# A selective-scan layer: new load order, diagonals from ScalarE's queue, gate behind the scan, 416 columns on VectorE

## The chip, the cores and the metric

The kernel runs on one core of one Trainium2 chip. The core has five engines: TensorE (PE; its weight loads are shown as PEld), VectorE (DVE), ScalarE (ACT), GpSimd (POOL) and SyncE (SP), which only issues transfers here. Each engine works through its own list of instructions in order and waits on semaphores for the others. Transfers between the chip's DRAM and the on-chip memory are issued from SP's or ScalarE's list and carried out by 16 DMA engines. The metric is the time of one execution on the device in microseconds; the number to be predicted is the median of the runs.

## What is computed

Two layers in a row on x of shape 32 x 96 x 56 x 56. Layer 0 is a convolution block (expand, depthwise, squeeze-and-excite, project). Layer 1, to which the change belongs, is a two-block selective scan over the 3136 tokens of each image. Cut to what matters:

```python
xs, z = jnp.split(h @ in_w, 2, axis=-1)            # h: normalised tokens, 192 channels each
xc = silu(causal 4-tap convolution of xs)
dbl = xc @ xproj_w                                  # 6 + 16 + 16 columns: dt, B, C
delta = softplus(dt @ dt_w + dt_b)
dA  = exp(delta[..., None] * A)                     # 192 channels x 16 states
dBx = delta[..., None] * Bm[:, :, None, :] * xc[..., None]
hstates[l] = dA[l] * hstates[l-1] + dBx[l]          # a scan along the tokens
y = einsum('blds,bls->bld', hstates, Cm) + Dp * xc
y = y * silu(z)
seq = seq + y @ out_w                               # two such blocks, then a batch norm
```

## The kernel before

**Units and tiles.** Each image's 3136 tokens are cut into four chunks of 784 (`LC`). One chunk in one of the two blocks is a unit; there are 256 units, in which the blocks alternate (the second runs three chunks behind the first). A unit has 192 channels x 16 states = 3072 rows, that is 24 tiles of 128 rows (`NT`). Tile t is (k, j, p): k, one of three groups of 64 channels (t // 8); j, one of four groups of four states; p, one of two halves of the channels. A tile's 128 rows are four states (`sg`) by 32 channels.

**Work on a tile.** `decay` (L921, ScalarE) makes dA = exp(delta x A) from the tile `deltab`, which holds delta of the channels copied to all four states. dBx comes in two ways. For three of four j GpSimd multiplies `ub` (delta x xc, likewise copied) with `B` (`inject`, L958, one instruction for both p). For j = 0 (`by_pe`: tiles 0, 1, 8, 9, 16, 17) TensorE computes it in 32 small matmuls (64 records in the trace) from `ut` and `diag`, a matrix with B on its diagonals (`fill`, L935). `scan` (L969, VectorE) runs the recurrence. The product with C is split by columns: the first `LP` = 400 tokens go to VectorE (`product`, L977, which reads a copy of C in PSUM made by ScalarE in `bring`, L946), the other 384 to GpSimd (`rest`, L985); one instruction covers both p. `reduce` (L1016, TensorE) sums over the states into `yps`, a single PSUM bank that `seed` (L1003, ScalarE) first fills with Dp x xc. After a group's eight tiles `gated` (L1027, VectorE) multiplies the sum with z.

**The order.** Everything is in one loop over steps `at`, one tile a step; `tc.manual_schedule()` keeps that order on every engine. At step `at` the loop issues the decay of the next tile (for j = 0 two to four steps ahead, in a borrowed `bx` buffer, L921 `bx<-deltab`), the GpSimd product of dBx of tile at + 4, the seed and reduction of tile at - 4, the gate of tile at - 5, the scan of tile `at`, the product of tile at - 1, TensorE's fill of tile at + 1, and then pieces of work for other units (`todo`: projections, normalisation and so on of the unit two ahead, the output of the unit before). The gate stands ahead of the scan: gate (at - 5), scan (at), product (at - 1).

**The loads.** `fetch`, at the end of each step, issues a tile's loads at fixed leads, all from SP's list: delta 9 steps ahead of its tile (L890, four pieces of 196 KB, tiles 0, 8 and 16), u 8 steps ahead (L890, four pieces of 196 KB, the same tiles), the diagonals 8 steps ahead of tile 0 (L894, one transfer of 120 rows x 12576 bytes), B 9 steps ahead (L899, four pieces of 98 KB, tiles 2, 4 and 6), C 5 steps ahead (L899, four pieces of 98 KB, tiles 0, 2, 4 and 6). I call them delta0, delta8, B2, C4 and so on by their tile. They read small DRAM buffers which the preparation of the unit has written: `bcd` (B and C), `deltad`, `ud`, and `bdiag`, into which six small transfers scatter B's values between zeros. There is one `diag` buffer, so its load waits until TensorE has filled tile 17 of the unit before; `deltab` and `ub` have two buffers, `B` three, `C` four.

**Semaphores of the loads.** The transfers issued by SP and ScalarE take eight semaphores in turn. Before a transfer is issued, its engine waits until the earlier transfer on the same semaphore has landed. The turns are dealt when the program is built. An engine that waits there issues nothing else of its list.

Of the kernel before, what the change touches and what calls it, by code (L numbers as in the profile page):

```python
# [19 lines left out]
B, C, H, W = 32, 96, 56, 56  # L20
# [4 lines left out]
NL, NS, DIN, RANK, KC = 2, 16, 192, 6, 4  # L25
LC = 784
HB = LC // 2
LP = 400
NQ = L // LC
RB = HB // W  # L30
DG = 8
# [3 lines left out]
NT = 2 * NB * SG  # L35
# [5 lines left out]
TB = 120  # L41
TOFF, TCOL, TSZ = (0, 120, 211, 301), (0, 120, 211, 302), (120, 91, 91, 91)
TW = TCOL[-1] + TSZ[-1]
TR = 8 * TW

PE_TILES = (0, 1)
FOLD = NCT - 1
# [12 lines left out]
def conv_mamba_kernel(ctx, tc, a, out):  # L60
    nc = tc.nc
    v, s, g, pe, sp = nc.vector, nc.scalar, nc.gpsimd, nc.tensor, nc.sync
# [41 lines left out]
    with ExitStack() as ph:  # L104
# [17 lines left out]
        def wtile(name, shape):  # L122
            return wts.tile(list(shape), F32, name=name, tag=name)
# [85 lines left out]
        diag = wtile("diag", [128, len(PE_TILES), 9, 32])  # L209
# [7 lines left out]
        for i in range(NHB):  # L217
            t = hp3.tile([128, H + 2, W + 2], F32, name=f"hpad{i}", tag=f"hpad{i}")
# [239 lines left out]
    with ExitStack() as ph:  # L458
# [17 lines left out]
        def wt(shape, tag, bufs, n):  # L476
            return work.tile(shape, F32, name=f"{tag}_{n}", tag=tag, bufs=bufs)
# [52 lines left out]
        for i in range(NL):  # L530
# [8 lines left out]
            for h in range(2):  # L539
                cols = slice(h * C, h * C + C)  # L540
                ps = bank(f"cw_{i}_{h}")
                for o in range(KC + 1):
                    to = ps[: C + 1, o * C : o * C + C]
# [16 lines left out]
        for h in range(2):  # L560
            for i in range(NL):
                to = wd[h * 64 + 2 * NS : h * 64 + 2 * NS + RANK, i, :, :]
# [6 lines left out]
        for k in range(NB):  # L569
            ps = bank(f"wf_{k}")  # L570
            for h in range(2):
                r = slice(h * 64, h * 64 + 64)
# [6 lines left out]
        g.memset(xn[C : C + 1, :], 1.0)  # L579
        none = once.tile([TB, TR + 2], F32, name="none", tag="none")  # L580
        v.memset(none, 0.0)
        zdram = ph.enter_context(tc.tile_pool(name="l1z", bufs=1, space=DRAM))
        bdiag = [zdram.tile([TB * (TR + 2)], F32, name=f"bdiag{i}", tag=f"bdiag{i}") for i in range(2)]
        for t in bdiag:
# [28 lines left out]
        def prepare(n):  # L613
# [148 lines left out]
            def scatter(h, e):  # L762
                bt, z = d["btt"], TSZ[-1]
                to = bdiag[n % 2].rearrange("(p r) -> p r", p=TB)[:, :TR].rearrange("p (e h x) -> p e h x", e=2, h=2)
                if e == 2:
# [107 lines left out]
        def place(t):  # L873
            k, r = divmod(t, 2 * SG)
            return k, r // 2, r % 2

        def fetch(at, tags):

            n, t = divmod(at, NT)
            if not 0 <= n < len(units):  # L880
                return
            k, j, p = place(t)
            d = data[n]
            for tag in tags:
                if tag in ("delta", "u"):
                    if j == 0 and p == 0:
                        to = d[tag, k] = wt([128, 2, LC], f"{tag}b", 2, f"{n}_{t}")
                        of = d[tag][2 * DB * k : 2 * DB * (k + 1), :].rearrange("(p m) l -> m p l", p=2)
                        for sg in (0, 2, 1, 3):
                            sp.dma_start(to[sg * DB : sg * DB + DB], of)  # L890
                elif tag == "diag":
                    if t == 0:
                        to = d["diag"] = wt([TB, TR], "diag", 1, n)
                        sp.dma_start(to, bdiag[n % 2][: TB * TR].rearrange("(p r) -> p r", p=TB))  # L894
                elif k == 0 and p == 0 and (tag, j) != ("B", PEJ):
                    to = d[tag, j] = wt([128, LC], tag, 3 if tag == "B" else 4, f"{n}_{t}")
                    c0 = "BC".index(tag) * NS + j * SN
                    for sg in (0, 2, 1, 3):
                        sp.dma_start(to[sg * DB : sg * DB + DB], d["bc"][c0 + sg : c0 + sg + 1, :].to_broadcast([DB, LC]))  # L899
# [3 lines left out]
        def by_pe(at):  # L903

            return place(at % NT)[1] == PEJ

        def lend(at):

            if by_pe(at) and at % 2 == 0:
                to = wt([128, 2, LC], "bx", 3, at)  # L910
                for p in range(2):
                    das[at + p] = to[:, p, :]

        def decay(at):

            n, t = divmod(at, NT)
            i, d = units[n][1], data[n]
            k, j, p = place(t)
            if not by_pe(at):
                das[at] = dpool.tile([128, 2 * 512], F32, name=f"da_{at}", tag="da")[:, :LC]  # L920
            s.activation(das[at], d["delta", k][:, p, :], AF.Exp, scale=acol[:, j, i, 2 * k + p : 2 * k + p + 1])  # L921
# [18 lines left out]
        def bring(at):  # L940
# [3 lines left out]
            if p == 1:  # L944
                cps[at] = cpool.tile([128, LP], F32, name=f"cp_{at}", tag="cp")
                s.copy(cps[at], data[n]["C", j][:, :LP])  # L946

        def beside(x):

            return x.unsqueeze(1).to_broadcast([128, 2, x.shape[-1]])  # L950

        def inject(at):

            n, t = divmod(at, NT)
            k, j, p = place(t)
            if p == 0 and j != PEJ:
                bx = wt([128, 2, LC], "bx", 3, at)
                g.tensor_mul(bx, data[n]["u", k], beside(data[n]["B", j]))  # L958
                for p in range(2):
                    bxs[at + p] = bx[:, p, :]  # L960

        def scan(at):

            n, t = divmod(at, NT)
            (c, i), d = units[n], data[n]
            k, j, p = place(t)
            if p == 0:
                hhs[at] = wt([128, 2, LC], "hh", 3, at)
            v.tensor_tensor_scan(  # L969
                hhs[at - p][:, p, :], das.pop(at), bxs.pop(at), state[i][:, t : t + 1] if c % NQ else 0.0,  # L970
                ALU.mult, ALU.add,
            )

        def product(at):

            if place(at % NT)[2] == 1:
                v.tensor_mul(hcs[at - 1][:, :, :LP], hhs[at - 1][:, :, :LP], beside(cps.pop(at)))  # L977

        def rest(at):
# [3 lines left out]
            if p == 1:  # L983
                hcs[at - 1] = wt([128, 2, LC], "hc", 3, at)
                g.tensor_mul(hcs[at - 1][:, :, LP:], hhs[at - 1][:, :, LP:], beside(data[n]["C", j][:, LP:]))  # L985

# [9 lines left out]
        def seed(at):  # L996

            n, t = divmod(at, NT)
            k, j, p = place(t)
            if j == 0 and p == 1:  # L1000
                i, d = units[n][1], data[n]
                yps[k] = ypool.tile([128, 512], F32, name=f"y_{n}_{k}", tag="y")
                s.activation(yps[k][:, :HB], d["xc"][:, k, :], AF.Copy, scale=dp[:, i, k, 1:2])  # L1003
# [25 lines left out]
        total = len(units) * NT  # L1029
# [12 lines left out]
        def ahead(at):  # L1042

            return (2, 1) if at % NT == 0 else (4, 3)
# [5 lines left out]
        with tc.manual_schedule():  # L1050
            for at in range(min(todo), max(todo) + 1):
                for m in (2, 4):
                    if 0 <= at + m < total and by_pe(at + m) and (at + m) % 2 == 0 and ahead(at + m)[0] == m:
                        lend(at + m)
                if 0 <= at + 4 < total:
                    inject(at + 4)
                for u, step in todo.get(at, ()):
                    if u < 0.05:
                        step()
                if 0 <= at - LAG < total:  # L1060
                    seed(at - LAG)
                if 0 <= at + 1 < total and not by_pe(at + 1):
                    decay(at + 1)
                for x in range(at, at + 5):
                    pair = x // 2 * 2
                    if 0 <= x < total and by_pe(x) and pair - ahead(pair)[x - pair] == at:
                        decay(x)
                if 0 <= at < total:
                    bring(at)
                for step in early.get(at, ()):  # L1070
                    step()
                if 0 <= at - LAG - 1 < total:
                    gated(at - LAG - 1)
                if 0 <= at < total:
                    scan(at)
                if 0 <= at - 1 < total:
                    product(at - 1)
                if 0 <= at - 2 < total:
                    save(at - 2)
                if 0 <= at < total:  # L1080
                    rest(at)
                if 0 <= at + 1 < total and by_pe(at + 1):
                    fill(at + 1)
                for u, step in todo.get(at, ()):
                    if 0.05 <= u < 0.08:
                        step()
                if 0 <= at - LAG < total:
                    reduce(at - LAG)
                for u, step in todo.get(at, ()):
                    if u >= 0.08:  # L1090
                        step()
                fetch(at + 9, ("delta",))
                fetch(at + 8, ("u", "diag"))
                fetch(at + 9, ("B",))
                fetch(at + 5, ("C",))


    with ExitStack() as ph:
# [76 lines left out]
```

## Time and profile before

| | |
|---|---|
| median of 3 runs | 18660.26 us (18648.78 to 18682.66) |
| the profiled execution | 18688.67 us, its span 18686.8 us |
| layer 0 | until about 3270 us |
| layer 1's units (first to last scan) | about 3476 to 18389 us |
| end (batch norm, output) | the last 290 us |
| DVE busy in the span | 16816.5 us (90%) |
| POOL busy in the span | 14627.0 us (78%) |
| ACT busy in the span | 14047.1 us (75%) |
| PE busy in the span | 15916.5 us (85%) |
| DMA in layer 1 | 0.76 of 16 engines, 186 GB/s |

The costliest groups of layer 1, from the page (line, engine, operation, out<-in, shapes, count | busy us, mean ns | idle time just before, and its releaser):

```profile
L958 POOL TENSOR_TENSOR bx<-ub,B 128x1568 f32<-128x1568 f32 x2304 | 8172.9, 3547 | 185.9 <-DMA B<-bcd 98.1
L969 DVE TENSOR_TENSOR_SCAN hh<-da,state,bx 128x784 f32<-128x784 f32 x3456 | 6312.4, 1839 | 54.4 <-ACT da L921 44.0
L985 POOL TENSOR_TENSOR hc<-hh,C 128x768 f32<-128x768 f32 x3072 | 5616.9, 1831 | 435.0 <-DVE hh L969 247.5
L921 ACT ACTIVATE da<-deltab,acol 128x784 f32<-128x784 f32 x4608 | 4243.3, 921 | 1046.4 <-DVE hh L969 1023.4
L977 DVE TENSOR_TENSOR hc<-hh,cp 128x800 f32<-128x800 f32 x3072 | 2952.1, 961 | 0.4 <-ACT cp L946 0.3
```

How to read it: the busy columns say how full an engine is over the whole span, so the first 3270 us, in which GpSimd does little, pull its 78% down. What a stall in layer 1 costs is read from a unit: which instruction waited, for whom, and what stood behind it on its engine. Transfers do not count as busy time; a wait of SP shows as a gap between its rows, or as a group of rows that takes longer than its pieces.

### The profile page before, as it was taken

The numbers are of one execution on the slowest core, as the hardware profiler recorded it, in microseconds if no ns is written. First come the engines' busy times: TensorE is split into PE (matmuls) and PEld (weight loads), VectorE is DVE, ScalarE is ACT, GpSimd is POOL, SyncE is SP. The second block draws the span as 40 slices with busy tenths as digits, with TensorE's granted clock in tenths as the row PEclk, the third lists the DMA queues.
The fourth block names the chain that finished last, engine by engine and source line by source line (L and its number), as shares of the span: only waits on it lengthen the run. The fifth ranks groups of instructions, "written<-read, shape, count | busy, mean of one in ns | idle before, by whom it ended". The sixth has DMA issues, their size and how long they took to land.

```text
span 18686.8 us, 503802 instructions
## 1 busy us (share of the span) xinstructions
PE 15916.5 (85%) x207422; PEld 8426.7 (45%) x207422; DVE 16816.7 (90%) x12627; ACT 14047.1 (75%) x26284; POOL 14627.0 (78%) x6382
## 2 busy tenths in 40 slices
PE   8999999888888888888888888888888888888882
PEld 4444444444444444444444444444444444444441
DVE  8888888699999999999999999999999999999993
ACT  4444444688888888888888888888888888888884
POOL 0000000599999999999999999999999999999994
PEclk9999999899999999999999999999999999999996
DMA  1000000577777777777777777777777777777778
GB/s 29 26 24 26 24 26 22 130 187 186 187 186 187 188 187 187 186 186 187 186 188 184 187 187 187 186 186 187 185 186 185 186 186 186 187 187 186 187 186 222
DMA packets 1615417, 2945.98 MB, mean 158 GB/s; under 512 B 696982, under 2 KB 910190, under 8 KB 1576006
## 3 DMA queue, kind: packets, MB, share of 16 engines
q1 hardware_dynamic: 1604470, 2875.15, 62.4%
q0 software_dynamic: 6656, 38.54, 1.0%
q8 instruction: 1627, 26.66, 0.6%
q14 instruction: 680, 5.57, 0.1%
q10 hardware_dynamic: 1984, 0.07, 0.0%
HBM read 2456.09 MB, written 455.82 MB: 156 GB/s over the span
## 4 chain that ended last, share of the span: by engine, by line
issue 25%; DMA 22%; PE 13%; DVE 12%; ACT 11%; SPq 10%; POOL 7%; POOLq 0%; ACTq 0%; DVEq 0%
DMA diag<-bdiag 8%; DVE hh L969 6%; PE bp L935 5%; SPq L899 4%; SPq L890 4%; DMA deltab<-deltad 4%; DMA ub<-ud 4%; DVE hc L977 3%; POOL bx L958 3%; DVE h L314 2%; DMA B<-bcd 2%; POOL hc L985 2%; ACT bx L921 2%; ACT da L921 2%; DMA C<-bcd 2%
## 5 line engine op out<-in xcount | busy, mean ns | idle before, releaser
L958 POOL TENSOR_TENSOR bx<-ub,B 128x1568 f32<-128x1568 f32 x2304 | 8172.9, 3547 | 185.9 <-DMA B<-bcd 98.1
L969 DVE TENSOR_TENSOR_SCAN hh<-da,state,bx 128x784 f32<-128x784 f32 x3456 | 6312.4, 1839 | 54.4 <-ACT da L921 44.0
L985 POOL TENSOR_TENSOR hc<-hh,C 128x768 f32<-128x768 f32 x3072 | 5616.9, 1831 | 435.0 <-DVE hh L969 247.5
L921 ACT ACTIVATE da<-deltab,acol 128x784 f32<-128x784 f32 x4608 | 4243.3, 921 | 1046.4 <-DVE hh L969 1023.4
L1016 PE MATMUL y<-hc,rel 128*32 128x392 f32 x24576 | 2866.3, 538 | 514.5 <-ACT y L1003 510.5
L935 PE MATMUL bp<-diag,ut 91*32 91x91 f32 (+1 forms) x98304 | 2980.0, 279 | 352.1 <-DVE hh L969 199.2
L935 PEld LDWEIGHTS bp<-diag,ut 91*32 91x32 f32 (+1 forms) x98304 | 2672.8, 123 | 1116.3 <-DVE hh L969 668.1
L977 DVE TENSOR_TENSOR hc<-hh,cp 128x800 f32<-128x800 f32 x3072 | 2952.1, 961 | 0.4 <-ACT cp L946 0.3
L389 POOL TENSOR_TENSOR x<-x,x 96x784 f32<-96x784 f32 x128 | 267.8, 2093 | 3079.1 <-ACT x L388 3035.7
L969 DVE TENSOR_TENSOR_SCAN hh<-bx,state,bp 128x784 f32<-128x784 f32 x1152 | 2118.0, 1839 | 395.2 <-PE bp L935 373.9
L701 PE MATMUL xs<-xn,wx 97*64 97x392 f32 x12288 | 2355.2, 525 | 36.8 <-ACT xc L712 36.0
L969 DVE TENSOR_TENSOR_SCAN hh<-da,bx 128x784 f32<-128x784 f32 x1152 | 2036.1, 1779 | 39.7 <-ACT da L921 36.3
L314 DVE SCALAR_TENSOR_TENSOR h<-hpad,hp,h 128x1568 f32<-128x1568 f32 x1024 | 2034.9, 1987 | 34.3
L946 ACT COPY cp<-C 128x400 f32<-128x400 f32 x3072 | 1523.8, 496 | 514.5 <-DVE hc L977 278.5
L921 ACT ACTIVATE bx<-deltab,acol 128x784 f32<-128x784 f32 x1536 | 1442.1, 939 | 239.3 <-DMA deltab<-deltad 233.2
L701 PEld LDWEIGHTS xs<-xn,wx 97*64 97x64 f32 x12288 | 834.0, 141 | 1504.5 <-issue 1376.1
L1016 PEld LDWEIGHTS y<-hc,rel 128*32 128x32 f32 x24576 | 608.8, 115 | 1495.4 <-ACT y L1003 979.9
L288 PE MATMUL dw<-hpad,diag 32*32 32x392 f32 x36864 | 1108.7, 519 | 47.2 <-issue 46.8
L386 PE MATMUL c<-h,w3s 128*96 128x392 f32 (+1 forms) x2560 | 970.0, 524 | 51.3 <-DVE w3s L371 51.3
L295 ACT ACTIVATE h<-dw,turn 128x392 f32<-128x392 f32 x512 | 340.0, 673 | 754.8 <-PE dw L288 754.8
L235 PE MATMUL c<-x,w 96*128 96x392 f32 x2048 | 790.5, 541 | 108.0 <-ACT hpad L237 85.9
L288 PEld LDWEIGHTS dw<-hpad,diag 32*32 32x32 f32 x36864 | 686.7, 105 | 416.2 <-issue 172.0
(192 smaller groups left out, 20394.2 us busy)
## 6 DMA issues: line engine op xcount, KB each, us to landing
deltab<-deltad SPq DMA_DIRECT2D x3072, 196.0 KB
ub<-ud SPq DMA_DIRECT2D x3072, 196.0 KB
C<-bcd SPq DMA_DIRECT2D x4096, 98.0 KB
diag<-bdiag SPq DMA_DIRECT2D x256, 1473.8 KB
B<-bcd SPq DMA_DIRECT2D x3072, 98.0 KB
deltad<-dl SPq DMA_DIRECT2D x512, 294.0 KB
ud<-us SPq DMA_DIRECT2D x1536, 98.0 KB
x<-in_x_dram SPq DMA_DIRECT2D x32, 1176.0 KB
```

Source lines behind the costliest of these rows:

```text
L288: pe.matmul(ps[r][to : to + 32, :HB], diag[src, n, t, :], hb[src, r0 : r0 + RB, dx : dx + W], start=t == 0, stop=t == 8, skip_group_check= ...
L314: v.scalar_tensor_tensor(acc, src, tap, acc, ALU.mult, ALU.add)
L386: pe.matmul(ps[:C, k, :HB], w3s[p, e, :], h[p, r, :], start=ct == 0, stop=ct == NCT - 1)
L701: pe.matmul(d["xs", k][h * 64 : h * 64 + 64, :HB], wx[:, i, o, k * 64 : k * 64 + 64], xn[:, o + h * HB : o + h * HB + HB], start=o == 0, s ...
L921: s.activation(das[at], d["delta", k][:, p, :], AF.Exp, scale=acol[:, j, i, 2 * k + p : 2 * k + p + 1])
L935: pe.matmul(ps[sg * DB : sg * DB + DB, o : o + z], d["ut", k][:z, b, h, p * DB : p * DB + DB], dg[:z, sg // 2, h, x : x + z, sg % 2], star ...
L946: s.copy(cps[at], data[n]["C", j][:, :LP])
L958: g.tensor_mul(bx, data[n]["u", k], beside(data[n]["B", j]))
L969: v.tensor_tensor_scan(hhs[at - p][:, p, :], das.pop(at), bxs.pop(at), state[i][:, t : t + 1] if c % NQ else 0.0, ALU.mult, ALU.add,)
L977: v.tensor_mul(hcs[at - 1][:, :, :LP], hhs[at - 1][:, :, :LP], beside(cps.pop(at)))
L985: g.tensor_mul(hcs[at - 1][:, :, LP:], hhs[at - 1][:, :, LP:], beside(data[n]["C", j][:, LP:]))
L1016: pe.matmul(yps[k][r0 : r0 + DB, :HB], rel, hc[:, p, h * HB : h * HB + HB], start=False, stop=j == SG - 1, skip_group_check=True,)
```

## The change

All edits are in layer 1's loop:

- The loads get a list, `BEFORE`, of (tile, kind, lead), issued in the list's order at each step. Leads in steps: u0 14 (was 8), delta0 9 (9), B2 11 (9), diagonals 7 (8), B4 11 (9), C0 6 (5), B6 11 (9), C2 6 (5), C4 6 (5), delta8 9 (9), C6 6 (5), u8 7 (8), u16 11 (8), delta16 9 (9). By the steps of the unit before, the order becomes u0 (10), delta0 and B2 (15), diagonals and B4 (17), C0 (18), B6 (19), C2 (20), C4 (22), delta8 (23), then C6 (0), u8 (1), u16 (5) and delta16 (7) of the unit itself. C4 now stands before delta8 and u16 before delta16.
- The diagonals are loaded by two transfers from ScalarE's list: the first 96 rows whole, and of the last 24 rows the part that is used (the first 240 of each 786 columns), 1269 KB together in place of 1474 KB.
- `gated` stands behind the step's scan: scan (at), gate (at - 5), product (at - 1).
- `LP` is 416: VectorE's products take 832 columns, GpSimd's 736, and ScalarE's copies of C 416.
- Nothing else of SP's list changes but its order and the diagonals' transfer, which leaves it.

```diff
--- before.py
+++ after.py
@@ -25,7 +25,7 @@
 NL, NS, DIN, RANK, KC = 2, 16, 192, 6, 4
 LC = 784
 HB = LC // 2
-LP = 400
+LP = 416
 NQ = L // LC
 RB = HB // W
 DG = 8
@@ -42,6 +42,7 @@
 TOFF, TCOL, TSZ = (0, 120, 211, 301), (0, 120, 211, 302), (120, 91, 91, 91)
 TW = TCOL[-1] + TSZ[-1]
 TR = 8 * TW
+TALL = 96
 
 PE_TILES = (0, 1)
 FOLD = NCT - 1
@@ -874,6 +875,13 @@
             k, r = divmod(t, 2 * SG)
             return k, r // 2, r % 2
 
+        BEFORE = [[] for _ in range(NT)]
+        for t, tag, m in (
+            (0, "u", 14), (0, "delta", 9), (2, "B", 11), (0, "diag", 7), (4, "B", 11), (0, "C", 6), (6, "B", 11), (2, "C", 6),
+            (4, "C", 6), (8, "delta", 9), (6, "C", 6), (8, "u", 7), (16, "u", 11), (16, "delta", 9),
+        ):
+            BEFORE[(t - m) % NT].append((m, (tag,)))
+
         def fetch(at, tags):
 
             n, t = divmod(at, NT)
@@ -891,7 +899,10 @@
                 elif tag == "diag":
                     if t == 0:
                         to = d["diag"] = wt([TB, TR], "diag", 1, n)
-                        sp.dma_start(to, bdiag[n % 2][: TB * TR].rearrange("(p r) -> p r", p=TB))
+                        of = bdiag[n % 2][: TB * TR].rearrange("(p r) -> p r", p=TB)
+                        s.dma_start(to[:TALL], of[:TALL])
+                        to, of = (x[TALL:].rearrange("p (a y) -> p a y", a=4)[:, :, : 2 * TSZ[0]] for x in (to, of))
+                        s.dma_start(to, of)
                 elif k == 0 and p == 0 and (tag, j) != ("B", PEJ):
                     to = d[tag, j] = wt([128, LC], tag, 3 if tag == "B" else 4, f"{n}_{t}")
                     c0 = "BC".index(tag) * NS + j * SN
@@ -1069,10 +1080,10 @@
                     bring(at)
                 for step in early.get(at, ()):
                     step()
+                if 0 <= at < total:
+                    scan(at)
                 if 0 <= at - LAG - 1 < total:
                     gated(at - LAG - 1)
-                if 0 <= at < total:
-                    scan(at)
                 if 0 <= at - 1 < total:
                     product(at - 1)
                 if 0 <= at - 2 < total:
@@ -1089,10 +1100,8 @@
                 for u, step in todo.get(at, ()):
                     if u >= 0.08:
                         step()
-                fetch(at + 9, ("delta",))
-                fetch(at + 8, ("u", "diag"))
-                fetch(at + 9, ("B",))
-                fetch(at + 5, ("C",))
+                for t, tags in BEFORE[at % NT]:
+                    fetch(at + t, tags)
 
 
     with ExitStack() as ph:
```

## The prediction

> **What bounds the kernel now.** I read the windows first, then the table of waits, then one unit's timelines. A unit is one chunk of 784 tokens in one of the two layers: 24 tiles (t = 0 to 23), one scan each; 256 units fill 3476 to 18389 us. The loads of unit n are issued while unit n-1 is scanned, so I count time from the start of unit n-1's scan of tile 17 and call it zero.
>
> ```profile
> 3500.00:18400.00 14900.00, 12729.94 (x162927) 6734.16 (x162927) 13928.55 (x10727) 12432.95 (x23817) 14292.70 (x6195) 0.92 0.76 186
> ```
>
> After the length the columns are the busy time of PE, PEld, DVE, ACT, POOL, the clock, DMA share and GB/s. VectorE (93%) and GpSimd (96%) are both nearly full, so a unit (58.27 us, mean distance of tile-17 scans) holds only 2 to 4 us of stalls. The waits, in us, times, longest:
>
> ```profile
> ACT bx L921 <- DMA deltab<-deltad: 233.2, 170, 2.9
> DVE hh L969 <- PE bp L935: 504.5, 551, 3.5
> DVE z L1027 <- PE y L1016: 305.4, 305, 3.5
> SPq L899 <- DMA diag<-bdiag: 1651.5, 254, 8.8
> ```
>
> The last is the start of the chain. SP's queue in one unit:
>
> ```profile
> 9039.55 1.81 SPq L890 DMA_DIRECT2D deltab<-deltad  x4
> 9041.41 2.70 SPq L890 DMA_DIRECT2D ub<-ud  x4
> 9044.20 0.38 SPq L894 DMA_DIRECT2D diag<-bdiag  x1
> 9044.78 2.87 SPq L899 DMA_DIRECT2D B<-bcd  x4
> 9048.53 1.48 SPq L733 DMA_DIRECT2D bcd<-bcs  x2
> 9050.38 8.79 SPq L899 DMA_DIRECT2D B<-bcd  x4
> 9059.26 2.64 SPq L899 DMA_DIRECT2D C<-bcd  x4
> 9062.00 1.77 SPq L899 DMA_DIRECT2D B<-bcd  x4
> 9063.88 2.91 SPq L899 DMA_DIRECT2D C<-bcd  x4
> 9066.88 1.78 SPq L890 DMA_DIRECT2D deltab<-deltad  x4
> ```
>
> In the built program every transfer of SP and ScalarE signals one of eight semaphores and first waits for the one before it on that semaphore. The second piece of B4 shares it with the diagonals: the group at 9050.38 sits 8.79 us until they have landed (issue 9044.20 + 13.71 in the chain of waits = 9057.91). Eighteen transfers later the last piece of delta8 (tiles 8 to 15) leaves, and ScalarE waits for it:
>
> ```profile
> 9044.92 0.19 ACT L994 COPY state<-hh 128x2 f32<-128x2 f32 x1
> 9072.71 0.95 ACT L921 ACTIVATE bx<-deltab,acol 128x784 f32<-128x784 f32 x1 [2.27 <-DMA deltab<-deltad]
> ```
>
> Behind that decay, in ScalarE's order, stand the y seed, the decay of tile 6 and the copies that tile 8's fill on TensorE needs. VectorE then stalls at tiles 6 and 8:
>
> ```profile
> 9042.28 1.84 DVE L969 TENSOR_TENSOR_SCAN hh<-bx,state,bp 128x784 f32<-128x784 f32 x1
> 9050.14 0.56 DVE L1027 TENSOR_TENSOR z<-z,y 128x392 f32<-128x392 f32 x1 [0.98 <-PE y L1016]
> 9075.08 1.85 DVE L969 TENSOR_TENSOR_SCAN hh<-da,state,bx 128x784 f32<-128x784 f32 x1 [1.20 <-ACT da L921]
> 9081.14 1.85 DVE L969 TENSOR_TENSOR_SCAN hh<-bx,state,bp 128x784 f32<-128x784 f32 x1 [1.57 <-PE bp L935]
> 9103.09 1.85 DVE L969 TENSOR_TENSOR_SCAN hh<-bx,state,bp 128x784 f32<-128x784 f32 x1
> ```
>
> This unit took 9103.09 - 9042.28 = 60.81 us with the decay at +30.43; the next one had it at 9130.90 (+27.81) and took 57.16. All units together, by the landing records: delta8 landed at +27.57 on average; landing before 27 the unit took 56.9 (83 units), 27 to 28 57.5 (49), 28 to 29 59.3 (59), 29 to 30 60.3 (34). Beyond 27 a microsecond of delta8 costs about 1.2 us of unit. So the change is judged by one question: when does delta8 land?
>
> **The diagonals to ScalarE's queue.** They stand after step 17's state copy: 2.64 us in the unit shown, 2.35 on average. SP issued them at +0.60. What they wait for (tile 17's fill, the scatters) is done by then. Two issues cost ScalarE 0.4 us each by SP's row; the 21 issues that ScalarE makes in the set-up take 0.27 to 1.08, so 0.8 to 1.3 us. Behind them stands tile 19's decay, whose result is wanted 2.3 us after the place of the issue (scan at 9047.32), and then a copy that waits 367.8/253 = 1.45 us for PE anyway. Cost nothing; without that cover up to 1.3 x 256 = 330 us. The first transfer is 96 rows of 12.6 KB. The same shape with an idle queue is the first load at the end:
>
> ```profile
> 18401.82 3.06 SPq L1111 DMA_DIRECT2D lp<-pred  x6
> 18409.48 3.00 ACT L1112 ACTIVATE lp<-lp,shbn,invbn 96x3136 f32<-96x3136 f32 x1 [4.32 <-DMA lp<-pred]
> ```
>
> 7.66 us to the reader (layer 0's 29 x loads, also 96x3136: 7.3 to 8.7). So the diagonals land at 2.35 + 7.7 = +10.05 (9.6 to 11), 3.4 earlier than now (+13.49 on average). Tile 0's fill, at about +15, no longer waits for them (102.2 us now).
>
> The Trainium skill (DMA: Bandwidth & Descriptors, "Anatomy of one DMA") gives 2.0 us plus bytes over 436 GB/s, an estimate of 4.8 us for this load; the 7.66 us row differs and decides. By the page delta8 would land near +26.7 and the median would be some 18300. The same page ("Issuing engines are not separate DMA queues") says that a second issuing engine saves only issue time, which speaks against a gain from the move; the 0.38 us row is all it would save.
>
> **What SP does meanwhile** decides the sign. In the changed program's list of waits the diagonals take their semaphore turn before the last piece of delta0 (123 units) or the first of B2 (125), although these are issued from step 15, earlier than step 17. The second, small transfer stands before B4's first piece. So SP stops there, at about -4, until +10.05, and then has to issue everything: 30 transfers, in the other half 29, up to delta8's last piece (delta0's rest, B2 4, B4 4, bcd 2, C0 4, B6 4, C2 4, C4 4, delta8 4). Before, 18 followed the stop: B2, one of B4 and the bcd store were already away, and C4 came behind delta8. u0's four pieces, moved to step 10, were ahead of the stop before as well.
>
> Price of one: 1.77/4 = 0.44 us in the fastest groups; 9.85/18 = 0.545 over the stretch now (average); mean issue 0.475 plus 0.045 between two = 0.52, which I take, as SP starts with free semaphores. Last piece to landing: 4.25 now. delta8 then lands at 10.05 + 29.5 x 0.52 + 4.25 = +29.6. Ends: 9.6 + 13.0 + 3.0 = +25.6 and 11 + 16.1 + 4.4 = +31.5. At 29.6 the unit takes 60.3 us by the units above: +2.0.
>
> Nearer loads: B2's last piece leaves at +12 and lands at 14.6, where GpSimd is ready at 13.7; its 1 us of idleness is paid from what it gains. C0 lands near +20, its product stands behind a scan ending at +22. No charge. u0 at step 10 makes SP wait about 2.1 us for the u store's landing, with u's third store behind it, used ten steps later: nothing.
>
> **The gate behind its scan.** The z wait is 305.4/305 = 1.0 us, mostly at tile 20 (1.07 a unit) and 0.14 at tile 12; the scan of 1.75 us hides it. Alone it could give 1.2 x 256 = 310 us. But tile 20 lies before tile 6 of the next unit, where delta8 sets the time: only the 0.14 remains. The gate ends one scan later; y's seed starts 1.3 to 2.4 us after it now, and follows the late decay anyway.
>
> **416 columns.** VectorE: (961 - 560)/(800 - 392) = 0.98 ns a column, 32 columns, 12 products: +0.38 us a unit; behind tile 8 lie five of twelve: +0.16. GpSimd: (3547 - 1831)/(1568 - 768) = 2.15 ns a column: -0.82 us a unit, off the path, as GpSimd waits where VectorE stalls. ScalarE's copies: under 0.2 us, inside its 2467 us of idle time.
>
> **Sum.** +2.0 + 0.16 - 0.14 = +2.0 us a unit, x 256 = +510. The profiled execution took 18688.7 (span 18686.8), so 19200; the median of the runs is 28 lower: 19170 us. Own range of this case: delta8 at 28.5 to 30.8, 18870 to 19500.
>
> **Rivals.** *The loads come in time* (faster): delta8 lands by +26. Then a unit is 56.9 - 1.07 - 0.14 + 0.38 = 56.1 by VectorE, or 56.98 (sum of GpSimd's rows: 9 x 3.547 + 12 x 1.831 + 3 x 1.03) - 0.82 + 0.37 of small idles = 56.5 by GpSimd: -1.8 x 256 gives 18210. It needs the burst at 0.44 us a piece and a 3 us landing. For it: the earlier diagonals and a queue without them. Against: 29.5 pieces at the measured pace. It decides below +27.9. *A draw*: the 11.5 further pieces just cost what the diagonals gain (3.4 us, 0.3 us each), delta8 near +27.6: 18560 to 18760; no group issues that fast. *ScalarE's issues are not covered*: forecast plus up to 330, 19500.
>
> **Chances.** Forecast 0.64, uncovered issues 0.06, draw 0.10, in time 0.20. Anything within 0.2% (about what a measurement of this kernel can tell from no change) takes 0.05 of the draw: faster 0.23, same 0.05, slower 0.72. The range, 18320 to 19480, leaves out the best of the fast cases and the uncovered issues.
>
> **What would show it.** SP's first row after the diagonals' issue should begin with their landing near +10; delta8's four should be issued near +24 to +25.5, behind C4's; the wait of the bx decay for deltab should grow from 233 us to some 800; VectorE's wait for PE bp should grow, and that for PE y shrink under 50. If SP doesn't stop, or delta8 lands by +27, I am wrong.

## The result, and the profile after

The changed kernel takes 18858.5 us (median of 4 runs, 18829.78 to 18874.62) against 18663.03 us of the kernel before beside it (4 runs, 18648.78 to 18682.66): a ratio of 1.0102, 95% interval 1.0085 to 1.012, so 1% slower. The forecast was 19170 us: the side is right and the time lies in the range, but the loss is 195 us and not 510.

The profiled execution is 18850.84 us, its span 18849.1 us. Its windows and the cores' view (columns as shown before):

```profile
3500.00:18400.00 14900.00, 12825.42 (x161572) 6789.32 (x161574) 13871.40 (x10617) 12374.14 (x23622) 13939.77 (x6130) 0.91 0.71 181
```

```profile
core 0: 18849.1 us, clock 0.903
```

VectorE and GpSimd are each less full than before (13871 and 13940 us of 14900, were 13929 and 14293). Both wait more. The table of waits, of VectorE, ScalarE and TensorE and then of SP's queue (us, times, longest):

```profile
PE y L1027 <- ACT y L1014: 792.9, 251, 5.4
DVE hh L980 <- PE bp L946: 715.5, 595, 3.6
ACT bx L932 <- DMA deltab<-deltad: 488.5, 234, 4.4
DVE hh L980 <- ACT da L932: 235.1, 391, 3.0
```

```profile
SPq L910 <- DMA diag<-bdiag: 1326.1, 128, 12.5
SPq L898 <- DMA diag<-bdiag: 1279.2, 123, 12.6
```

The wait of the `bx` decay for delta8 went from 233.2 us in 170 units to 488.5 in 234, and VectorE's wait for TensorE's `bp` from 504.5 to 715.5. VectorE's wait for `y` (305.4 before) is no longer among the listed waits. SP now waits 2605 us for the diagonals, 10.4 a unit, in the two places where the turn of the semaphore falls. One unit (its predecessor's scan of tile 17 starts at 9050.69, our zero), SP's queue:

```profile
9045.04 2.75 SPq L898 DMA_DIRECT2D deltab<-deltad  x4
9058.58 3.56 SPq L910 DMA_DIRECT2D B<-bcd  x8
9062.24 0.83 SPq L734 DMA_DIRECT2D bcd<-bcs  x2
9063.17 1.77 SPq L910 DMA_DIRECT2D C<-bcd  x4
9065.04 2.42 SPq L910 DMA_DIRECT2D B<-bcd  x4
9067.56 4.45 SPq L910 DMA_DIRECT2D C<-bcd  x8
9072.11 1.78 SPq L898 DMA_DIRECT2D deltab<-deltad  x4
```

Nothing leaves between 9047.79 and 9058.58, then 30 pieces in one go, delta8 as the last four, as forecast. But the silence ends at +7.9 and not at +10.05, because ScalarE's transfers left early:

```profile
9050.46 0.19 ACT L1005 COPY state<-hh 128x2 f32<-128x2 f32 x1
9050.56 0.26 ACT L648 ACTIVATE va<-var,epsc 112x7 f32<-112x7 f32 x1
9050.85 0.18 ACT L649 ACTIVATE var<-va 112x7 f32<-112x7 f32 x1
9051.06 0.15 ACT L650 ACTIVATE var<-var 112x7 f32<-112x7 f32 x1
9051.14 0.18 ACT L652 COPY xn<-tail 97x3 f32<-97x3 f32 x1
9051.21 0.31 ACTq L903 DMA_DIRECT2D diag<-bdiag  x1
9051.22 0.92 ACT L932 ACTIVATE da<-deltab,acol 128x784 f32<-128x784 f32 x1
9051.56 0.79 ACTq L905 DMA_DIRECT2D diag<-bdiag  x1
9052.07 0.50 ACT L957 COPY cp<-C 128x416 f32<-128x416 f32 x1
9052.50 0.19 ACT L1005 COPY state<-hh 128x2 f32<-128x2 f32 x1
9052.59 0.92 ACT L932 ACTIVATE da<-deltab,acol 128x784 f32<-128x784 f32 x1
```

In ScalarE's list the two transfers stand after the state copy shown at 9052.50. The row marked ACTq, the engine's sequencer, has the first at 9051.21, when the decay that stands three instructions ahead of it is only starting. The queued decay, C copy and state copy are executed afterwards. So the issue is 1.3 us ahead of its place, in this unit and on average (182 of 242 units have such a state copy: it starts at +1.98, the issue is at +0.71), and costs ScalarE no time: the next decay follows at once. In all 242 units the transfer leaves within 0.6 us, 0.14 on average, of the start of the `var` activation (L650, here 9051.06), the last one ahead of it in the list whose wait is still open: it needs the result of the activation before it. The 60 units without the state copy, in which one instruction less is queued, show the same 0.12 us. So in these traces that wait dates the issue, and not the number of instructions queued.

The table averages over some 240 middle units, from the records of the traces; its times count from the start of the scan of tile 17 in the unit before. "Behind" is the number of pieces from the one at which SP stops to delta8's last, both included, by the semaphores in the traces (the prediction's 18 before and 30 or 29 after leave out the stopped one); the kernels E1 to E13 follow in the next section.

| kernel | diagonals issued | landed | behind | delta8 landed | unit, us |
|---|---|---|---|---|---|
| before | 0.60 | 13.5 | 19 | 27.57 | 58.27 |
| after | 0.70 | 8.45 | 30.5 | 28.02 | 58.96 |
| E1, diagonals on SP's queue | 1.7 | 10.5 | 20 | 25.12 | 56.50 |
| E13, E1 with delta8 before C4 | 2.0 | 11.0 | 16 | 23.39 | 56.20 |
| E3, delta8 before C4 | 0.8 | 8.95 | 26.5 | 26.6 | 57.34 |
| E5, issue one step later | 4.8 | 12.45 | 28.5 | 31.08 | 62.11 |
| E8, the list alone | 1.7 | 12.74 | 19 | 26.93 | 57.71 |

In every row delta8 landed less diagonals landed less some 4.35 us (last piece to landing) is the number of pieces times 0.50 to 0.52 us. E3, for one: (26.6 - 8.95 - 4.35) / 26.5 = 0.50.

### The profile page after: what moved, and what is told of

It reads as the page before. It is cut to its first block, busy times and chain, and to the rows that moved or that the text cites. A ratio compares the mean times of both kernels' runs of the same rounds, so it can differ in the third digit from the quotient of the medians.

```text
span 18849.1 us, 503930 instructions
## 1 busy us (share of the span) xinstructions
PE 16135.9 (86%) x207422; PEld 8545.1 (45%) x207422; DVE 16914.1 (90%) x12627; ACT 14100.2 (75%) x26284; POOL 14443.3 (77%) x6382
## 5 line engine op out<-in xcount | busy, mean ns | idle before, releaser
L996 POOL TENSOR_TENSOR hc<-hh,C 128x736 f32<-128x736 f32 x3072 | 5411.1, 1762 | 689.2 <-DVE hh L980 471.5
L1027 PE MATMUL y<-hc,rel 128*32 128x392 f32 x24576 | 2906.7, 546 | 855.6 <-ACT y L1014 851.2
L988 DVE TENSOR_TENSOR hc<-hh,cp 128x832 f32<-128x832 f32 x3072 | 3065.9, 998 | 0.1
L702 PE MATMUL xs<-xn,wx 97*64 97x392 f32 x12288 | 2488.3, 551 | 3.8 <-ACT xc L713 3.5
L957 ACT COPY cp<-C 128x416 f32<-128x416 f32 x3072 | 1577.5, 514 | 293.9 <-DVE hc L988 256.4
L236 PE MATMUL c<-x,w 96*128 96x392 f32 x2048 | 831.5, 564 | 96.8 <-ACT hpad L238 74.6
L980 DVE TENSOR_TENSOR_SCAN hh<-bx,bp 128x784 f32<-128x784 f32 x384 | 682.6, 1778 | 239.2 <-PE bp L946 222.9
```

The lines of the kernel that those rows point to most:

```text
L702: pe.matmul(d["xs", k][h * 64 : h * 64 + 64, :HB], wx[:, i, o, k * 64 : k * 64 + 64], xn[:, o + h * HB : o + h * HB + HB], start=o == 0, s ...
L980: v.tensor_tensor_scan(hhs[at - p][:, p, :], das.pop(at), bxs.pop(at), state[i][:, t : t + 1] if c % NQ else 0.0, ALU.mult, ALU.add,)
L1027: pe.matmul(yps[k][r0 : r0 + DB, :HB], rel, hc[:, p, h * HB : h * HB + HB], start=False, stop=j == SG - 1, skip_group_check=True,)
```

## The experiments

E1 to E5 take back or move one part of the changed kernel, E11 issues the diagonals from a third engine, E13, E9 and E10 start from E1, and E8 and G1 put one part into the kernel before. All were timed beside the kernel before (18710 to 18717 us there), and each ratio is to that.

**E1: the diagonals back on SP's queue, all else as changed.**

```diff
-                        s.dma_start(to[:TALL], of[:TALL])
+                        sp.dma_start(to[:TALL], of[:TALL])
...
-                        s.dma_start(to, of)
+                        sp.dma_start(to, of)
```

> The changed kernel with the diagonals' two transfers issued from SP's queue again (same leads, same order); nothing else differs. In the built program their semaphore turns then come after delta0 and B2, and the first transfers that wait for them are C0's first two pieces, so 19 transfers stand between the stop and delta8's last piece, not 29 or 30. Theory (SP's stop behind the diagonals makes delta8 late, and a late delta8 stalls VectorE at tiles 6 and 8): delta8 lands near +23 us after the start of tile 17's scan of the unit before (28.0 now), the wait of the bx decay for deltab falls from 488 us to under 60, a unit takes 56.3 to 56.7 us (58.96 now), about 18200 to 18300 us. Rival 1 (the gate behind its scan delays the y seed and with it tile 8's fill): the stall at tile 8 stays, 18800 to 18900. Rival 2 (416 columns on VectorE): also 18800 to 18900.

18240.06 us, ratio 0.9751 (0.9736 to 0.9765). One edit turns a loss of 1% into a gain of 2.5%: the queue of the diagonals is what makes the change slow. Delta8 landed at +25.1, later than expected. SP's queue in one unit (zero is 8984.49) and its waits say why:

```profile
8984.76 1.71 SPq L910 DMA_DIRECT2D B<-bcd  x4
8986.83 0.30 SPq L903 DMA_DIRECT2D diag<-bdiag  x1
8987.63 0.84 SPq L905 DMA_DIRECT2D diag<-bdiag  x1
8989.91 1.71 SPq L910 DMA_DIRECT2D B<-bcd  x4
8991.73 0.82 SPq L734 DMA_DIRECT2D bcd<-bcs  x2
8995.22 1.70 SPq L910 DMA_DIRECT2D C<-bcd  x4
```

```profile
SPq L910 <- DMA diag<-bdiag: 784.5, 263, 5.1
```

```profile
ACT bx L932 <- DMA deltab<-deltad: 57.4, 60, 2.4
```

SP still stops for the diagonals (the gap before 8995.22), but only after six more transfers: B4 and the store to `bcd` are away, B2 and delta0 too, and the stop costs 784.5 us in all in place of 2605. The diagonals land 2 us later than in the changed kernel and delta8 lands 3 us earlier, since 20 pieces have to go from the stop on and not 30.5. The wait of the `bx` decay for delta8 (the second line) falls from 488.5 to 57.4 us, and VectorE's stall at tile 8 from 1.99 to 0.37 us a unit. Their early landing was worth less than the place of the stop.

**E2: the gate ahead of the scan, in the changed kernel.**

```diff
+                if 0 <= at - LAG - 1 < total:
+                    gated(at - LAG - 1)
                 if 0 <= at < total:
                     scan(at)
-                if 0 <= at - LAG - 1 < total:
-                    gated(at - LAG - 1)
```

> The changed kernel with the gate ahead of its step's scan again. Theory: delta8's landing sets the unit, so the wait for y returns at tile 20 and disappears in the slack before tile 6: within 0.3% of the changed kernel, 18830 to 18920 us. Rival 1 (the gate behind the scan is what costs): 18650 to 18750, and PE's wait for the y seed falls from 793 to about 480 us.

18858.84 us, ratio 1.0084 (1.0067 to 1.0101), the same as changed. VectorE waits 1.06 us for `y` at tile 20 again, and its stalls at tiles 6 and 8 shrink from 0.69 and 1.99 us to 0.25 and 1.37: where delta8 sets the time a wait only changes its place.

**E3: delta8 before C4 in the list, the diagonals on ScalarE's queue.**

```diff
-            (4, "C", 6), (8, "delta", 9), (6, "C", 6), (8, "u", 7), (16, "u", 11), (16, "delta", 9),
+            (8, "delta", 10), (4, "C", 6), (6, "C", 6), (8, "u", 7), (16, "u", 11), (16, "delta", 9),
```

> The changed kernel with delta8 issued ahead of C4 (both at step 22). Theory: four transfers fewer between the stop and delta8's last piece, 4 x 0.52 = 2.1 us: delta8 lands near +26 instead of +28.0, a unit takes 56.4 to 57.0 us, 18200 to 18400 us in all. C4, now behind delta8, lands near +27, before its copy needs it. Rivals 1 and 2: the order of these loads changes nothing, 18800 to 18900.

18473.9 us, ratio 0.9873 (0.9859 to 0.9888), 74 us above the expected range. Four pieces fewer ahead of delta8 take 1.4 us from its landing (the table) and 1.6 us from the unit: with the stop in place, the number of pieces behind it decides.

**E4: 400 columns again, in the changed kernel** (`LP = 400`).

> The changed kernel with 400 columns on VectorE. Theory: VectorE's five products between tile 8 and tile 17 lose 0.03 us each and GpSimd's work is off the path: 0 to 60 us faster than the changed kernel, 18790 to 18860. Rival 2 (the columns cost their full 12 x 0.037 us a unit): 114 us faster, about 18740.

18850.84 us, ratio 1.0076 (1.0061 to 1.0091): the 416 columns cost nothing that can be told.

**E5: the diagonals issued one step later.**

```diff
-            (0, "u", 14), (0, "delta", 9), (2, "B", 11), (0, "diag", 7), (4, "B", 11), (0, "C", 6), (6, "B", 11), (2, "C", 6),
+            (0, "u", 14), (0, "delta", 9), (2, "B", 11), (0, "diag", 6), (4, "B", 11), (0, "C", 6), (6, "B", 11), (2, "C", 6),
```

> The changed kernel with the diagonals issued one step later (after step 18's work instead of step 17's), nothing else. It separates two rules for when ScalarE's DMA instruction leaves. Theory (its sequencer sends it as soon as the semaphores of the instructions before it are satisfied, ahead of the execution of queued activations): the last wait ahead of it is that of the B/C/delta copy for PE, so it leaves near +4.8 us from the start of tile 17's scan; landing +12.4, SP stops until then, delta8 lands near +32, and at 1.45 us of unit for each us of delta8 beyond 28 the unit takes some 64.5 us: 20200 to 20500 us. Rival (it leaves only when everything before it in ScalarE's list has been executed, as the forecast put it): +6.3, landing +13.9, delta8 +33.5, unit near 66.8: 20700 to 21000 us. Rival 2 (delta8's landing doesn't set the unit, something else of the change does): within 1% of the changed kernel, 18700 to 19050.

19675.92 us, ratio 1.0519 (1.0498 to 1.054). The place of the issue is the theory's: +4.8 on average. One unit on ScalarE (zero is 9627.36):

```profile
9628.60 0.50 ACT L957 COPY cp<-C 128x416 f32<-128x416 f32 x1
9629.24 0.92 ACT L932 ACTIVATE da<-deltab,acol 128x784 f32<-128x784 f32 x1
9632.03 0.48 ACT L731 COPY bcs<-bc 128x392 f32<-128x392 f32 x1 [1.87 <-PE bc L727]
9632.17 0.31 ACTq L903 DMA_DIRECT2D diag<-bdiag  x1
9632.41 0.35 ACT L680 ACTIVATE sx_t<-ct,rs 112x96 f32<-112x96 f32 x1
9632.52 0.79 ACTq L905 DMA_DIRECT2D diag<-bdiag  x1
9632.64 0.81 ACT L680 ACTIVATE sx_t<-ct,rs 112x96 f32<-112x96 f32 x3
```

The copy `bcs` waits 1.87 us for TensorE, and the transfer does not pass it while it waits: it leaves 0.14 us after the copy starts. The four `sx_t` activations, which stand ahead of it in the list and show no wait, it does pass. The time was overestimated, 20200 to 20500 expected: with the diagonals' turn later, two more pieces leave ahead of SP's stop, so that delta8 landed at 31.08 and not 32, and a unit grew by (62.11 - 58.96) / (31.08 - 28.02) = 1.03 us for each us of delta8 between these two kernels, not by the 1.45 which I had fitted over the units of one.

**E11: the diagonals from GpSimd's list** (`g.dma_start` in both places), which takes no turn on the eight semaphores.

> The changed kernel with both transfers of the diagonals issued by GpSimd instead of ScalarE, so that they take no turn on the eight semaphores that SP's and ScalarE's transfers share. Theory (SP's stop until the diagonals' landing makes delta8 late, not the landing itself): SP doesn't stop, delta8 leaves behind C4 before +20 and lands by +25; GpSimd pays some 2 us a unit for two issues (its own stores in the last stage take 1.04 to 1.38 us each) and becomes the bound: unit 56.8 to 58.2, 18290 to 18660 us. Rival (the change is slow because the diagonals and the loads share the DMA engines, or because of the list's order): delta8 stays near +28 and the time near 18850 or above.

18589.48 us, ratio 0.994 (0.9925 to 0.9954), within the expected range. SP has no wait for the diagonals left. Delta8 landed at +26.65, not by +25: without the stop SP is held up by the step's order, by GpSimd's freeing of the B buffers (1305.7 us) and by the landing of the `bcd` store (660.1 us). And the diagonals themselves come late (zero is 9129.87 in this unit):

```profile
9130.58 3.50 POOL L969 TENSOR_TENSOR bx<-ub,B 128x1568 f32<-128x1568 f32 x1
9134.04 1.74 POOL L996 TENSOR_TENSOR hc<-hh,C 128x736 f32<-128x736 f32 x1
9135.72 0.10 POOL L666 MEMSET xn<- 97x3 f32 x1
9135.76 0.57 POOL L903 DMA_DIRECT2D diag<-bdiag  x1
9136.33 0.61 POOL L905 DMA_DIRECT2D diag<-bdiag  x1
```

```profile
PE bp L946 <- DMA diag<-bdiag: 452.4, 226, 4.7
```

GpSimd issues them only when its products are done, at +6.6 on average, and with 8.3 us to landing TensorE waits for them in 226 units, 2.0 us each. So this run shows that without turns SP does not stop for the diagonals; how fast the loads could then be, it does not show, as SP's small loads beside them are slow (last section).

**E13: E1 with delta8 before C4** (both edits above).

> The changed kernel with the diagonals on SP's queue (as in e1) and delta8's four pieces ahead of C4's in the list (as in e3). Theory: with the stop gone delta8 lands at +25 on average and only some units are late; 4 pieces less ahead of it bring it to +23, so that the late units vanish and GpSimd's 56.2 us of work bound every unit: 18180 to 18240 us, up to 0.3% below e1. Rival (something other than delta8's landing still costs in e1): no change, within 0.1% of e1's 18240. C4 four pieces later: its product stands far behind, no charge.

18167.84 us, ratio 0.9713 (0.9698 to 0.9727), the fastest of all, 2.9% below the kernel before. Delta8 landed at +23.4; it came after +26 in 65 of 242 units of E1, and here in 7.

**E9: E1 with 400 columns.**

> The changed kernel with the diagonals on SP's queue (as in e1) and 400 columns of the C products on VectorE instead of 416. Theory: where the loads come in time GpSimd bounds the unit (56.16 of 56.50 us busy in e1); 12 products with 32 columns more at 2.15 ns give it 0.82 us: unit 57.1 to 57.4, 18400 to 18480 us, so that the 416 columns are worth some 200 us there, against the 8 us that they were worth in the changed kernel as it is, where delta8 bounds. Rival (the loads bound e1 too): 18220 to 18300.

18245.27 us, ratio 0.9752 (0.9735 to 0.9768): missed. I had expected GpSimd to bound the unit, because the sum of its rows, 56.16 us, nearly fills E1's 56.50. In E9 that sum is 57.14 us and the unit 56.51, so the sum is more than the time there is. GpSimd's rows overlap, as its timeline in E9 shows:

```profile
9000.71 3.59 POOL L969 TENSOR_TENSOR bx<-ub,B 128x1568 f32<-128x1568 f32 x1
9004.24 1.83 POOL L996 TENSOR_TENSOR hc<-hh,C 128x768 f32<-128x768 f32 x1
9006.00 3.52 POOL L969 TENSOR_TENSOR bx<-ub,B 128x1568 f32<-128x1568 f32 x1
9009.46 1.85 POOL L996 TENSOR_TENSOR hc<-hh,C 128x768 f32<-128x768 f32 x1
```

The distances of the starts are 3.53, 1.76 and 3.46 us, 0.06 to 0.07 us less than the durations, some 1.3 us over the 21 long rows of a unit. Without the overlap GpSimd's work is 55.9 us in E9 and 55.1 in E1: it had room for the 0.82 us of the 32 columns, while VectorE won 0.38 by the forecast's price. What bounds a unit of E1 or E13, in which GpSimd is idle for 1.4 and 1.1 us, no run settles.

**E10: E1 with the gate ahead of the scan** (the edit of E2).

> The changed kernel with the diagonals on SP's queue (as in e1) and the gate ahead of its step's scan, as before the change. Theory (the forecast's: the gate's move is worth the 1.0 to 1.2 us of the z wait wherever delta8's landing does not set the unit): VectorE waits again about 1 us a unit for PE's y at tile 20, unit 57.2 to 57.7 against e1's 56.50, 18410 to 18550 us, where the same undoing changed nothing in the changed kernel itself (58.87 against 58.96). Rival (the move is worth nothing anywhere, since GpSimd or the loads take up what VectorE gains): within 0.3% of e1, 18190 to 18300.

18442.54 us, ratio 0.9856 (0.984 to 0.9873). The wait at tile 20 is back:

```profile
DVE z L1038 <- PE y L1027: 308.9, 294, 2.4
```

The unit is 57.28 us, 0.79 more than E1's. So the gate's move is worth 1.05% here and nothing in the changed kernel.

**E8: the list alone in the kernel before** (diagonals in one transfer on SP's queue, gate first, 400 columns).

> The kernel before with the new list of loads alone: the diagonals in one transfer on SP's queue at the list's place, the gate ahead of the scan, 400 columns. Theory (most of e1's gain of 470 us is the list with the stop gone, the gate the rest, the columns nothing): delta8 near +25.5, unit 57.0 to 57.7, 18370 to 18550 us. Rival (the list gives nothing by itself, the gain is the gate's): 18650 to 18750. Rival 2 (the list gives all of it): 18200 to 18300.

18555.7 us, ratio 0.9916 (0.9901 to 0.9931), 6 us above the expected range. The diagonals took 11.0 us in one transfer, in E1 8.8 us in two, and delta8 came at +26.93, so that a part of the units is still late. E10 is E8 with two transfers and 416 columns; by E9 the columns are worth nothing there, which leaves the 0.6% between E8 and E10 to the split (it also drops 205 KB of unused columns), though no run changed it alone.

**G1: the gate alone in the kernel before.**

> The kernel before with the gate behind its step's scan and nothing else. The forecast's term: where delta8 sets the unit only 0.14 of the 1.2 us remains, -36 us: 18650 to 18700 beside a kernel before at 18710. Rival (the move gives its whole 1.0 to 1.2 us a unit): 18400 to 18460. Rival 2 (y's seed, which follows later, makes it slower): above 18740.

18632.66 us, ratio 0.9958 (0.9944 to 0.9972): -0.42%, some 80 us and 17 us below the expected range, between the term of the forecast (36) and the full wait. So the forecast's 0.14 us a unit for the gate was too small in the kernel before (80 us are some 0.3 a unit).

So the change without its move to ScalarE is three gains: the list 0.8%, the split 0.6% (by the difference of two runs), the gate 1.05%; the move takes them all back and 1% more.

## Why the prediction was right in sign and wrong in size

**What held, number by number.** SP stops at the semaphore turn until the diagonals land (E11, without turns, has no such stop; E1, with the turns elsewhere, has it elsewhere). The first transfer takes 7.6 to 7.7 us in the changed kernel, E2, E4 and E5, and 8.0 in E3 (forecast 7.66). Then the 30 or 29 transfers behind the stopped one go at 0.519 to 0.522 us (0.52), and delta8's last piece takes 4.3 us to land (4.25). ScalarE's two issues cost it nothing: the decay of tile 19 starts at +2.26 on average, before at +2.28. The wait for `y` went to nothing and gave nothing (E2), and the columns gave nothing (E4). TensorE's wait for the diagonals is gone.

**The step that failed** is "They stand after step 17's state copy: 2.64 us in the unit shown, 2.35 on average", taken as the time of the issue. It is the place in ScalarE's list, and I read it as if the engine's list were executed strictly one after the other. The runs show an issue at +0.70: ScalarE's sequencer sends the transfer when the instructions ahead of it have no wait left, past work that is still queued (the changed kernel: 0.14 us after the start of `var`, the last that waits; E5: past four `sx_t`, not past the waiting copy). The average was also misread: by the records of the kernel before the state copy starts at +2.04 (182 units), so of the 1.65 us between the forecast's issue and the measured one some 1.3 are the sequencer's lead and 0.3 this reading. The Trainium skill (Perfetto Trace Analysis, "Per-instruction lifecycle: what the profiler-reported window actually captures") says as much: an activation is pushed into a queue and the sequencer goes on to the next instruction, while a transfer is the sequencer's own work. I did not weigh that page. The traces here agree, with a lead of 1.3 us on average. The forecast's signs moved with it: in the unit shown SP's first row came at +7.9 and not near +10, delta8's four left from +22.3 on average and not +24 to +25.5, and the wait of the `bx` decay grew to 488.5 us and not to some 800.

**What that is worth.** With +0.70 in the forecast's own sum the diagonals land at 0.70 + 7.7 = 8.4 and delta8 at 8.4 + 29.5 x 0.52 + 4.25 = +28.0 (measured 28.02), 0.45 later than before; at 1.2 us each and with +0.16 and -0.14 that is +0.56 us a unit, +143 us, 18800. The opposite check: between the changed kernel and E5, whose edit moves only the issue (and with the turns two pieces to the other side of the stop), the ratio rises from 1.0102 at +0.70 to 1.0519 at +4.80. At the forecast's +2.35 a straight line between these two gives 1.027, about 19160 us. The forecast had said 19170, so its other terms, taken together, were near enough, and as far as such a line can tell the one mis-sized term makes the miss.

**Small remainders.** The unit is 0.69 us longer and the corrected sum explains 0.56. The gate's 0.14 and the columns' 0.16 were each too small for E2 and E4 to show in the changed kernel; in the kernel before the gate gave more (G1). The rest, about 0.1 us a unit, is open.

**The rivals.** "The loads come in time" needed a faster burst; what makes it come true is not the pace but fewer pieces behind the stop: E1's 56.50 us and E13's 56.20 are the 56.1 to 56.5 us that this rival gave as the unit, and 18168 to 18240 us lie about its 18210. Some of that agreement is luck: its 56.5 us by GpSimd summed rows that overlap (E9). "ScalarE's issues are not covered" falls: they take sequencer time alone. The "draw" was close in mechanism, delta8 at +28.02 against its +27.6, with the gain of the earlier landing nearly eaten by the 11.5 more pieces.

## What to carry to other kernels

When a transfer is moved to another issuing queue, look first at whose turn it takes: here two queues shared eight semaphores in turn, so a load on ScalarE's queue stopped SP's at a place that neither list shows, and the cost is the number of pieces still to be issued behind that place times the price of one. In these runs an issue from ScalarE was dated not by what executes ahead of it, but by the last wait ahead of it in its list. And a wait off the path of the moment is not worthless: the gate's move gave nothing while delta8 was late, and 1% once it came in time.

## What the runs showed of the hardware

- ScalarE's transfers of the diagonals leave 1.3 us ahead of the state copy that stands before them in its list (after), and show as rows of 0.31 and 0.79 us of its sequencer; GpSimd's leave in turn with its work and take 0.57 and 0.61 us of the engine (E11).
- The 120-row transfer of the diagonals takes 12.9 us (before) and 11.0 us (E8), and the 96 whole rows with a narrower rest 8.8 us on the same queue (E1) and 7.6 us from ScalarE's queue (after), where nothing of SP's was issued beside it. The Trainium skill (DMA: Bandwidth & Descriptors, "Why a DMA increments its semaphore by 16 and not by 1") has a transfer run on the largest number of engines up to 16 that divides its rows: 15 for 120 rows, 16 for 96, so 8 rows an engine against 6. The landing records fit this: of the 16 steps of the semaphore one comes about 0.6 us after the issue of the 120 rows and the others after 8.3 us or more (E8), and for the 96 rows none comes before 5.6 us (E1). The ratio of 8.8 to 11.0 is near that of 6 to 8, but the bytes of the first transfer fell to 0.80 as well, so no run tells the two causes apart. The 4.8 us that the forecast worked out from the same page is far from all of these; the page gives that fit for transfers that GpSimd issues.
- B4's pieces, issued right behind the diagonals on the same queue, landed after 5.7 to 6.3 us on average (E1). A second queue did not spare a small load that: in E11, with the diagonals issued by GpSimd at +6.6, C0's pieces, which SP issued at +7.8 to +9.5, took 7.4 to 8.0 us to land; in E1, issued with the diagonals landed, the same pieces took 2.3 to 2.5. This agrees with the rule that the forecast quoted (same page, "Issuing engines are not separate DMA queues").
- TensorE's granted clock was by and large lower in slower kernels: 0.885 (E5), 0.903 (after), 0.920 (before), 0.932 (E13). It does not follow the time alone: G1, faster than the kernel before, has 0.915. Whether it is a cause or a consequence no run tells apart.
